# Deformable sampling: gathered rows as TensorE's stationary side against small corner-weight matrices, in place of weighting on VectorE

## Chip, cores, metric

One core of one Trainium2 chip. The metric is the device time of one execution in microseconds (us), the median of several. Every timed execution leaves its span and its mean granted TensorE clock as well. Engines: PE is TensorE's matmul, PEld its weight load, DVE VectorE, ACT ScalarE, POOL GpSimd, SP SyncE. The granted clock is the share of full speed at which TensorE's array was let run, 1 being full speed. In the traces of the kernel before each record of it is 1 or 0.5; other values are means over time. An array at 1 is called warm here, one at 0.5 cold. PSUM is the memory that TensorE writes its sums to; a tile of 128 x 512 float32 in it is called a bank here.

## The reference, cut to what matters

Four images of 256 x 64 x 64 go through four layers, all in float32. Layer 0 is a deformable convolution: for each of 4096 pixels, 4 groups of 64 channels and 9 points, it computes a position, reads the four corners around it, and sums them with bilinear weights and a softmax mask.

```python
def _forward(x, ...):                      # layer 0
    y    = leaky_relu(bn1(conv1x1(x)))
    inp  = y.transpose(0, 2, 3, 1)
    xp   = inp @ inproj_w.T + inproj_b                     # what is sampled
    t    = leaky_relu(bn(depthwise3x3(y)))
    offset, mask = t @ off_w.T + off_b, softmax(t @ mask_w.T + mask_b)   # 9 points a group
    samp = tap(x0, y0, (1-wx)*(1-wy)) + tap(x0+1, y0, wx*(1-wy)) + tap(x0, y0+1, (1-wx)*wy) + tap(x0+1, y0+1, wx*wy)
    dout = (samp * mask).sum(points) @ outproj_w.T + outproj_b
    x2   = bn2(inp + dout)
    ...                                    # squeeze and excitation, feed-forward
# layer 1: linear attention with 5x5 depthwise aggregation; layer 2: 3x3 convolution; layer 3: attention over a pooled image
```

Layer 1's 25-tap aggregation runs on DVE: in layer 1 of the second stage (5,321 to 6,758 us) POOL waits 385.8 us for multiplies on DVE, 77.0 us at the longest, and in seven of the eight longest waits 22 to 33 of the 25-tap instructions run meanwhile.

## The kernel before

The sampling of image n+1 runs beside the later layers of image n: `sample` yields after each tile and the layers yield weights, and so much of the layers is issued beside each tile, in an order that is fixed when the program is built. This is the part that changes (cut):

```python
    def sample(self, n, ssum):
        ...
                for j in range(4):                               # a tile of 128 pixels
                    i = 4 * h + j
                    pd = self.ps2.tile([P, 512], F32, name="pd", tag="ps2")
                    for pr in range(KT):                         # pairs of groups
                        for p3 in range(PT // 3):                # three points at a time
                            g = self.gp.tile([P, 2, 3, 256], F32, name="g", bufs=4)
                            for g2 in range(2):
                                for p in range(3):               # pixels in partitions
                                    nc.gpsimd.indirect_dma_start(out=g[:, g2, p, :], ...)     # L391
                            gw = self.gp.tile([P, 12, 2, 64], F32, name="gw")
                            nc.vector.tensor_tensor(gw..., g..., wt..., ALU.mult)             # L397
                            for q in range(12):
                                nc.tensor.matmul(pd[:, pr * P:(pr + 1) * P],                  # L403
                                                 gw[:, q].rearrange("p g c -> p (g c)"), self.ident, ...)
                    nc.scalar.copy(dT[:, :, j * P:(j + 1) * P], ...)                          # L405
                    yield 1
```

A gather brings the four corners of one point for 128 pixels. DVE multiplies by the weights; TensorE sums, with the weighted rows as the stationary side (loaded as weights) and a 128-column identity as the moving side. A float32 product is recorded as two matmuls with a load each, so the 9,216 products stand in the profile as 18,432.

## Time and profile before

| | before |
|---|---|
| time, median of three runs (lowest to highest) | 12,077.8 us (12,076.2 to 12,086.0) |
| span of the profiled execution | 11,965.6 us |
| PE, DVE, POOL busy | 63%, 52%, 43% |
| mean granted TensorE clock | 0.783 |

The execution of this profile was 112 us shorter than the timed runs.

From the page: busy time by engine, then the span in 40 slices. A digit is the busy share of a slice in tenths (PE), or the granted clock in tenths of full speed (PEclk).

```profile
PE 7491.4 (63%) x32548; PEld 5103.6 (43%) x32548; DVE 6180.6 (52%) x6605; ACT 1463.0 (12%) x2377; POOL 5185.3 (43%) x4614
PE   3545555584366887494557797495546797832696
PEclk6677677796678898696777898697777898965699
```

The clock row is 6 or 7 wherever sampling fills TensorE (0.69 as a mean over image 0's sampling). The stages and waits are in the prediction.

### The profile page before, as it was taken

To read this page: it belongs to the slowest core of one execution; us is meant where nothing else is said; L and a number is where in the kernel's file an instruction comes from. 1 tells how busy PE (TensorE), PEld (TensorE's weight loads), DVE (VectorE), ACT (ScalarE), POOL (GpSimd) and SP (SyncE) were. 2 spreads that over 40 slices of the span, in tenths; PEclk is the share of its full clock that TensorE was granted. 3 is DMA by queue.
4 is the path that set the end of the run, shared out by engine and by line. 5 is a ranking of instruction groups with operands and counts; after the bars stand their busy time and mean duration, and the time that the engine had idled before them with its cause. 6 is when DMAs were issued, how large, how long until landed. Compare 5 with 4: busy or idle time off the path is not lost. (4 is left out here: it accounts for less than half of the span.)

```text
span 11965.6 us, 85517 instructions
## 1 busy us (share of the span) xinstructions
PE 7491.4 (63%) x32548; PEld 5103.6 (43%) x32548; DVE 6180.6 (52%) x6605; ACT 1463.0 (12%) x2377; POOL 5185.3 (43%) x4614
## 2 busy tenths in 40 slices
PE   3545555584366887494557797495546797832696
PEld 2444444353344455353443455344433456421235
DVE  5322222558857233548868323638776423399713
ACT  1000000121010012011100012111110002221002
POOL 0777774355557361445565452245665543000000
PEclk6677677796678898696777898697777898965699
DMA  3333333322222122322221221322222212100000
GB/s 111 109 96 101 97 97 94 103 80 67 65 70 80 53 82 71 114 75 64 67 84 61 67 66 62 110 88 74 74 75 68 76 55 64 56 0 0 0 10 14
DMA packets 451708, 837.94 MB, mean 70 GB/s; under 512 B 222432, under 2 KB 234208, under 8 KB 449504
## 3 DMA queue, kind: packets, MB, share of 16 engines
q0 software_dynamic: 221184, 604.27, 16.7%
q1 hardware_dynamic: 230112, 228.21, 5.9%
q8 instruction: 255, 4.18, 0.1%
q14 instruction: 157, 1.29, 0.0%
HBM read 731.41 MB, written 100.71 MB: 70 GB/s over the span
## 5 line engine op out<-in xcount | busy, mean ns | idle before, releaser
L391 POOL DMA_INDIRECT g<-tab,ixl x4608 | 5184.6, 1125 | 4870.5 <-DVE gw L397 2309.2
L403 PE MATMUL pd<-ident,gw 128*128 128x128 f32 x18432 | 2777.1, 318 | 1545.1 <-DVE gw L397 1019.4
L403 PEld LDWEIGHTS pd<-ident,gw 128*128 128x128 f32 x18432 | 2661.6, 231 | 1727.3 <-DVE gw L397 1052.4
L397 DVE TENSOR_TENSOR gw<-g,wtl 128x1536 f32<-128x1536 f32 x768 | 1348.3, 1758 | 2581.5 <-DMA g<-tab,ixl 1600.0
L150 DVE SCALAR_TENSOR_TENSOR av<-pd,w,av 128x1024 f32<-128x1024 f32 x1152 | 1481.5, 1286 | 1.5
L150 DVE SCALAR_TENSOR_TENSOR ak<-pd,w,ak 128x1024 f32<-128x1024 f32 x1152 | 1480.2, 1285 | 0.4
L606 PE MATMUL ps<-xp,w 128*128 128x512 f32 x2304 | 993.9, 593 | 2.6 <-ACT xp L597 2.6
L521 PE MATMUL pt<-ident,ak 128*128 128x128 f32 x256 | 86.2, 407 | 981.8 <-ACT ak L537 973.8
L606 PEld LDWEIGHTS ps<-xp,w 128*128 128x128 f32 x2304 | 435.3, 189 | 551.8 <-issue 549.2
L405 ACT COPY dT<-pd 128x256 f32<-128x256 f32 x128 | 47.6, 372 | 4113.1 <-PE pd L403 2372.5
L610 DVE TENSOR_TENSOR x<-x,ps 128x512 f32<-128x512 f32 x64 | 44.0, 688 | 878.7 <-PE ps L606 797.1
L456 PE MATMUL ps<-x2f,f 128*128 128x512 f32 x1024 | 468.7, 616 | 40.5 <-ACT hm L457 28.1
L521 PEld LDWEIGHTS pt<-ident,ak 128*128 128x128 f32 x256 | 50.0, 213 | 990.7 <-ACT ak L537 982.1
L462 PE MATMUL ps<-hm,f 128*128 128x512 f32 x1024 | 446.7, 594 | 2.2 <-ACT hm L457 2.2
L313 PE MATMUL ps<-mw,t 128*128 128x108 f32 x512 | 101.0, 378 | 479.8 <-DVE t L134 430.9
L496 PE MATMUL ps<-xn,qw 128*128 128x512 f32 x768 | 379.8, 622 | 11.3 <-ACT xn L116 7.7
L685 PEld LDWEIGHTS ps<-gt,pT 128*128 128x128 f32 x2048 | 294.4, 222 | 110.6 <-issue 52.7
L456 PEld LDWEIGHTS ps<-x2f,f 128*128 128x128 f32 x1024 | 200.4, 198 | 297.0 <-issue 246.6
L685 PE MATMUL ps<-gt,pT 128*128 128x128 f32 x2048 | 298.5, 306 | 37.4 <-DVE pT L682 20.0
L150 DVE SCALAR_TENSOR_TENSOR t<-y,vec,t 128x1024 f32<-128x1024 f32 x256 | 315.7, 1287 | 0.1
L134 DVE SCALAR_TENSOR_TENSOR hm<-hm 128x512 f32<-128x512 f32 x256 | 172.8, 692 | 273.2 <-ACT hm L457 259.2
L668 PE MATMUL s<-ph,th 128*128 128x512 f32 x512 | 312.2, 703 | 0.0
(187 smaller groups left out, 6595.7 us busy)
## 6 DMA issues: line engine op xcount, KB each, us to landing
g<-tab,ixl POOLq DMA_INDIRECT x4608
x<-in_x SPq DMA_DIRECT2D x64, 512.0 KB
tab<-xo SPq DMA_DIRECT2D x512, 64.0 KB
y<-yc SPq DMA_DIRECT2D x32, 512.0 KB
yb<-y SPq DMA_DIRECT2D x32, 512.0 KB
x<-x SPq DMA_DIRECT2D x32, 512.0 KB
x2f<-x SPq DMA_DIRECT2D x32, 512.0 KB
ybf<-y SPq DMA_DIRECT2D x32, 512.0 KB
```

The source lines that it names most:

```text
L134: self.nc.vector.scalar_tensor_tensor(out, z, SLOPE, z, ALU.mult, ALU.max)
L150: nc.vector.scalar_tensor_tensor(acc, s, wt, acc, ALU.mult, ALU.add)
L391: nc.gpsimd.indirect_dma_start(out=g[:, g2, p, :], out_offset=None, in_=table, in_offset=bass.IndirectOffsetOnAxis(ap=ix[:, i, at:at + 1], ...
L397: nc.vector.tensor_tensor(gw.rearrange("p s g c -> p g s c"), g.rearrange("p g q (s c) -> p g (q s) c", c=64), wt[:, i].rearrange("p (g s) ...
L403: nc.tensor.matmul(pd[:, pr * P:(pr + 1) * P], gw[:, q].rearrange("p g c -> p (g c)"), self.ident, start=p3 == 0 and q == 0, stop=p3 == 2 ...
L456: nc.tensor.matmul(ps, f1[:, k, m * P:(m + 1) * P], x2[:, k], start=k == 0, stop=k == KT - 1)
L462: nc.tensor.matmul(ps, f2[:, k, m * P:(m + 1) * P], hm[:, k], start=k == 0, stop=k == 4 * KT - 1)
L496: nc.tensor.matmul(ps, qw[:, k, i * P:(i + 1) * P], xn[:, k], start=k == 0, stop=k == KT - 1)
L521: nc.tensor.transpose(pt[:, 0, j], kv[:, j * P:(j + 1) * P], self.ident)
L606: nc.tensor.matmul(ps, w[:, k, t, m * P:(m + 1) * P], xp[:, k, 8 * b + t // 3:8 * b + t // 3 + 8, t % 3:t % 3 + W], start=i == 0, stop=i = ...
L668: nc.tensor.matmul(s[:, i], tv[:, 4 * b + j], ph[:, i * 512:(i + 1) * 512], start=True, stop=True)
L685: nc.tensor.matmul(ps[:, 0:P], pT[:, m], gt[:, m], start=m == 0, stop=m == 7)
```

## The change

The intent is to take DVE out of the path from a gather to the sum. The samples are laid out by (pixel, point), so that the 128 rows of one gather are some 14 or 15 pixels with 9 points each. The gathered rows, unweighted, become the stationary side. The moving side is a matrix of 128 rows by 32 columns (16 pixels x 2 image rows of the corner): it holds a sample's corner weight in its pixel's column and zero elsewhere. One product then weights and sums. DVE builds only these matrices, which need no gathered data.

```diff
-                            g = self.gp.tile([P, 2, 3, 256], F32, name="g", bufs=4)      # 6 gathers a tile
-                            ... gw = g * wt on DVE, 128 x 1536 ...
-                            for q in range(12):
-                                nc.tensor.matmul(pd[:, pr * P:(pr + 1) * P], gw[:, q]..., self.ident, ...)
+                    wm = self.gp.tile([P, PT, 8, OB], F32, name="wm")                    # OB = 16
+                    nc.vector.tensor_tensor(wm, con("own")..., wt[:, :, 8 * i:8 * i + 8]..., ALU.mult)    # L394
+                    pd = self.ps2.tile([P, 2, 2, P], F32, name="pd", tag="ps2")
+                    for g2 in range(2):
+                        g = self.gp.tile([P, PT, 256], F32, name="g", bufs=4)            # 9 gathers a tile
+                        for j in range(PT):
+                            nc.gpsimd.indirect_dma_start(out=g[:, j, :], ...)            # L404
+                        for j in range(PT):
+                            for x in range(2):
+                                nc.tensor.matmul(pd[:, g2, :, OUT0[j]:OUT0[j] + OB], g[:, j, x * P:(x + 1) * P],   # L409
+                                                 wm[:, j, 4 * g2 + 2 * x:4 * g2 + 2 * x + 2, :], ...)
+                    for s in range(2):
+                        nc.scalar.copy(dT[64 * s:64 * s + 64, ...], pd[64 * s:64 * s + 64, :, s, :])              # L415
```

(Cut: the index and weight layouts in memory, the projection over 4 x 128 rows in place of 2 x 128, buffers merged to make room, and the share of the layers beside a step halved, as a step is half a tile's work.)

More of the change, by code (lines that the diff above doesn't have):

```diff
@@ L27 @@
 SLOPE = 0.01
-SHARE = 56
+SHARE = 28
 EPS_BN = 1e-5
@@ L47 @@
 NVEC = _at
+OB = 16
+OUT0 = [min(P * j // PT, P - OB) for j in range(PT)]
 ROWS = {"inproj_b": (0, C), "offmask_b": (C, 3 * Q), "g_b": (C + 3 * Q, P)}
@@ L52 @@
 CON = {"bd": (0, P), "oh": (P, 16), "bx": (P + 16, Q), "by": (P + 16 + Q, CT * Q),
-       "gi": (P + 16 + Q + CT * Q, Q), "sel": (P + 16 + 2 * Q + CT * Q, 4 * P)}
-NCON = P + 16 + 2 * Q + CT * Q + 4 * P
+       "gi": (P + 16 + Q + CT * Q, Q), "sel": (P + 16 + 2 * Q + CT * Q, 4 * P),
+       "own": (P + 16 + 2 * Q + CT * Q + 4 * P, PT * OB)}
+NCON = P + 16 + 2 * Q + CT * Q + 4 * P + PT * OB
 class Net:
@@ L164, in setup @@
         nc.sync.dma_start(self.rows, a["rows"])
-        self.ow = cp.tile([P, KT, C], F32, name="ow")
+        self.ow = cp.tile([P, G, C], F32, name="ow")
         nc.sync.dma_start(self.ow, a["outproj_wT"])
@@ L179, in setup @@
         self.inv, self.sh = inv, sh
-        self.w5 = cp.tile([P, 6, 25], F32, name="w5")
+        self.w5 = self.vec("dw5", n=150).rearrange("p (m t) -> p m t", t=25)
         nc.vector.tensor_tensor(
-            self.w5, self.vec("dw5", n=150).rearrange("p (m t) -> p m t", t=25),
-            self.vec("agg_pw_w", n=6).unsqueeze(2).to_broadcast([P, 6, 25]), ALU.mult)
+            self.w5, self.w5, self.vec("agg_pw_w", n=6).unsqueeze(2).to_broadcast([P, 6, 25]), ALU.mult)
         self.b5 = cp.tile([P, 6], F32, name="b5")
@@ L193, in setup @@
         self.x2_d = [dt([P, KT, HW], F32, name=f"x2{n}") for n in im]
-        self.w_d = [dt([P, NT, Q * 4], F32, name=f"wt{n}") for n in im]
-        self.i_d = [dt([P, NT, Q], I32, name=f"ix{n}") for n in im]
+        self.w_d = [dt([NCH, P * PT, CT * G * 4], F32, name=f"wt{n}") for n in im]
+        self.i_d = [dt([NCH, P * PT, CT * G], I32, name=f"ix{n}") for n in im]
         self.w2_d = dt([P, KT, 9, C], F32, name="w2")
@@ L342, in coordinates @@
         nc.vector.scalar_tensor_tensor(t1, f0[:, 1], float(TX), f0[:, 0], ALU.mult, ALU.add)
-        ix = bp.tile([P, CT, Q], I32, name="ix")
-        nc.vector.tensor_tensor(ix, tq(t1), self.con("gi").unsqueeze(1).to_broadcast([P, CT, Q]), ALU.add)
-        nc.sync.dma_start(self.i_d[n][:, c * CT:(c + 1) * CT, :], ix)
+        ix = bp.tile([P, PT, CT, G], I32, name="ix")
+        nc.vector.tensor_tensor(
+            ix.rearrange("p q t g -> p t g q"), t1.rearrange("p (t g q) -> p t g q", g=G, q=PT),
+            self.con("gi").rearrange("p (g q) -> p g q", q=PT).unsqueeze(1).to_broadcast([P, CT, G, PT]), ALU.add)
+        nc.sync.dma_start(self.i_d[n][c].rearrange("(p q) f -> p (q f)", q=PT), ix.rearrange("p q t g -> p (q t g)"))
         mg = ml.rearrange("p t (g q) -> p (t g) q", q=PT)
@@ L356, in coordinates @@
         mf = ml.rearrange("p t q -> p (t q)")
-        wt = bp.tile([P, M, 2, 2], F32, name="wt")
+        wt = bp.tile([P, PT, CT * G, 2, 2], F32, name="wt")
+        fq = lambda v: v.rearrange("p (f q) -> p f q", q=PT)
         for xt, wx in ((0, w0[:, 0]), (1, loc[:, 0])):
@@ L361, in coordinates @@
             for yt, wy in ((0, w0[:, 1]), (1, loc[:, 1])):
-                nc.vector.tensor_tensor(wt[:, :, xt, yt], ax, wy, ALU.mult)
-        nc.sync.dma_start(self.w_d[n][:, c * CT:(c + 1) * CT, :].rearrange("p t q -> p (t q)"),
-                          wt.rearrange("p m a b -> p (m a b)"))
+                nc.vector.tensor_tensor(wt[:, :, :, xt, yt].rearrange("p q f -> p f q"), fq(ax), fq(wy), ALU.mult)
+        nc.sync.dma_start(self.w_d[n][c].rearrange("(p q) f -> p (q f)", q=PT),
+                          wt.rearrange("p q f a b -> p (q f a b)"))
     def sample(self, n, ssum):
@@ L372, in sample @@
         for c in range(NCH):
-            ix = sp.tile([P, CT, Q], I32, name="ixl")
-            nc.sync.dma_start(ix, self.i_d[n][:, c * CT:(c + 1) * CT, :])
-            wt = sp.tile([P, CT, 4 * Q], F32, name="wtl")
-            nc.sync.dma_start(wt, self.w_d[n][:, c * CT:(c + 1) * CT, :])
+            ix = sp.tile([P, PT, CT * G], I32, name="ixl")
+            nc.sync.dma_start(ix, self.i_d[n][c].rearrange("(j p) f -> p j f", p=P))
+            wt = sp.tile([P, PT, CT * G * 4], F32, name="wtl")
+            nc.sync.dma_start(wt, self.w_d[n][c].rearrange("(j p) f -> p j f", p=P))
             for h in range(2):
@@ L380, in sample @@
                 nc.sync.dma_start(yb, self.y_d[n][:, :, b * 512:(b + 1) * 512])
-                dT = sp.tile([P, KT, 512], F32, name="dT")
-                for j in range(4):
-                    i = 4 * h + j
-                    pd = self.ps2.tile([P, 512], F32, name="pd", tag="ps2")
-                    for pr in range(KT):
-                        for p3 in range(PT // 3):
-                            g = self.gp.tile([P, 2, 3, 256], F32, name="g", bufs=4)
-                            for g2 in range(2):
-                                for p in range(3):
-                                    at = (2 * pr + g2) * PT + 3 * p3 + p
-                                    nc.gpsimd.indirect_dma_start(
-                                        out=g[:, g2, p, :], out_offset=None, in_=table,
-                                        in_offset=bass.IndirectOffsetOnAxis(ap=ix[:, i, at:at + 1], axis=0))
-                            gw = self.gp.tile([P, 12, 2, 64], F32, name="gw")
-                            at = 12 * p3
-                            nc.vector.tensor_tensor(
-                                gw.rearrange("p s g c -> p g s c"), g.rearrange("p g q (s c) -> p g (q s) c", c=64),
-                                wt[:, i].rearrange("p (g s) -> p g s", g=G)[:, 2 * pr:2 * pr + 2, at:at + 12]
-                                .unsqueeze(3).to_broadcast([P, 2, 12, 64]), ALU.mult)
-                            for q in range(12):
-                                nc.tensor.matmul(pd[:, pr * P:(pr + 1) * P], gw[:, q].rearrange("p g c -> p (g c)"),
-                                                 self.ident, start=p3 == 0 and q == 0, stop=p3 == 2 and q == 11)
-                    nc.scalar.copy(dT[:, :, j * P:(j + 1) * P], pd[:, 0:C].rearrange("p (k t) -> p k t", k=KT))
@@ new lines, in sample @@
+                dT = sp.tile([P, G, 512], F32, name="dT", bufs=1)
+                for i in range(8 * h, 8 * h + 8):
+                    pr, j4 = i % 2, i // 2 % 4
+                    wm = self.gp.tile([P, PT, 8, OB], F32, name="wm")
+                    nc.vector.tensor_tensor(
+                        wm, self.con("own").rearrange("p (j o) -> p j o", o=OB).unsqueeze(2).to_broadcast([P, PT, 8, OB]),
+                        wt[:, :, 8 * i:8 * i + 8].unsqueeze(3).to_broadcast([P, PT, 8, OB]), ALU.mult)
+                    pd = self.ps2.tile([P, 2, 2, P], F32, name="pd", tag="ps2")
+                    for g2 in range(2):
+                        g = self.gp.tile([P, PT, 256], F32, name="g", bufs=4)
+                        for j in range(PT):
+                            at = 2 * i + g2
+                            nc.gpsimd.indirect_dma_start(
+                                out=g[:, j, :], out_offset=None, in_=table,
+                                in_offset=bass.IndirectOffsetOnAxis(ap=ix[:, j, at:at + 1], axis=0))
+                        for j in range(PT):
+                            for x in range(2):
+                                nc.tensor.matmul(pd[:, g2, :, OUT0[j]:OUT0[j] + OB], g[:, j, x * P:(x + 1) * P],
+                                                 wm[:, j, 4 * g2 + 2 * x:4 * g2 + 2 * x + 2, :],
+                                                 start=g2 + j + x == 0, stop=g2 == 1 and j == PT - 1 and x == 1,
+                                                 skip_group_check=True)
+                    for s in range(2):
+                        hs = slice(64 * s, 64 * s + 64)
+                        nc.scalar.copy(dT[hs, 2 * pr:2 * pr + 2, j4 * P:(j4 + 1) * P], pd[hs, :, s, :])
@@ L406, in sample @@
                     yield 1
-                x2 = sp.tile([P, KT, 512], F32, name="x2")
                 for m in range(KT):
                     po = self.ps2.tile([P, 512], F32, name="po", tag="ps2")
-                    for k in range(KT):
-                        nc.tensor.matmul(po, self.ow[:, k, m * P:(m + 1) * P], dT[:, k], start=k == 0, stop=k == KT - 1)
-                    nc.vector.tensor_tensor(x2[:, m], po, yb[:, m], ALU.add)
-                    nc.scalar.activation(x2[:, m], x2[:, m], AF.Identity, bias=self.sh[:, 4 + m:5 + m],
+                    for k in range(G):
+                        nc.tensor.matmul(po, self.ow[:, k, m * P:(m + 1) * P], dT[:, k], start=k == 0, stop=k == G - 1)
@@ L414, in sample @@
+                    nc.vector.tensor_tensor(yb[:, m], po, yb[:, m], ALU.add)
+                    nc.scalar.activation(yb[:, m], yb[:, m], AF.Identity, bias=self.sh[:, 4 + m:5 + m],
                                          scale=self.inv[:, 4 + m:5 + m], accum_out=ssum[:, m, b:b + 1])
-                nc.sync.dma_start(self.x2_d[n][:, :, b * 512:(b + 1) * 512], x2)
+                nc.sync.dma_start(self.x2_d[n][:, :, b * 512:(b + 1) * 512], yb)
     def feedforward(self, n, ssum, x1):
@@ L775, in arrays @@
         "gi": np.broadcast_to((q // PT) * TY * TX + TX + 1, (P, Q)),
+        "own": ((P * np.arange(PT)[None, :, None] + p[:, None, None]) // PT
+                == np.array(OUT0)[None, :, None] + np.arange(OB)[None, None]).reshape(P, -1),
         "sel": (p[:, None, None] == 16 * np.arange(4)[None, :, None] + p[None, None] // 8).reshape(P, -1),
@@ L786, in arrays @@
         "offmask_wT": lhsT(np.concatenate([w[l0 + "off_w"], w[l0 + "mask_w"]])),
-        "outproj_wT": lhsT(w[l0 + "outproj_w"]),
+        "outproj_wT": asc(np.tile(w[l0 + "outproj_w"].T.reshape(G, 64, C).transpose(1, 0, 2), (2, 1, 1))),
         "se_down_wT": lhsT(w[l0 + "se_down_w"]),
```

## The prediction

> **What bounds the kernel now.** I first cut the span into its stages, by where each image's gathers and later layers start and end, and read the busy time of each engine in each. Columns: window, length, busy us and count on PE, PEld, DVE, ACT and POOL, granted clock, DMA share, GB/s.
>
> ```profile
> 233.00:2003.00 1770.00, 891.81 (x4855) 805.90 (x4856) 459.19 (x389) 54.75 (x101) 1253.82 (x1152) 0.69 0.33 99
> 2003.00:2287.00 284.00, 106.30 (x556) 90.62 (x555) 172.25 (x221) 29.73 (x41) 97.98 (x90) 0.66 0.37 117
> 2287.00:4697.00 2410.00, 1671.88 (x7488) 1120.57 (x7488) 1341.83 (x1374) 316.02 (x525) 1214.84 (x1063) 0.82 0.22 68
> 4697.00:5049.00 352.00, 145.63 (x640) 116.64 (x640) 194.28 (x272) 49.74 (x69) 101.61 (x91) 0.69 0.39 125
> 10204.00:11966.00 1762.00, 1091.67 (x3132) 543.95 (x3132) 1023.78 (x1183) 292.55 (x467) 0.00 (x0) 0.78 0.03 11
> ```
>
> Image 0 is sampled with no later layers beside it (1770 us), image 1 is prepared (284), then three times the sampling of an image runs beside the feed-forward and layers 1 to 3 of the one before (2410, 2418, 2391), with a preparation between (352, 346), and the last image's later layers run alone (1762). With the prologue of 233 that is the span of 11,966. The reader is to see that a stage with sampling takes 650 us more than the same layers alone, though no engine is busy more than 70% of it. Next, the layer-1 part of a stage and of the last image, same columns:
>
> ```profile
> 2551.00:3990.00 1439.00, 817.30 (x3991) 594.50 (x3990) 1034.15 (x920) 165.34 (x286) 848.36 (x726) 0.74 0.24 73
> 10438.00:11375.00 937.00, 397.39 (x1029) 178.18 (x1028) 812.17 (x789) 146.30 (x242) 0.00 (x0) 0.64 0.00 2
> ```
>
> 500 of the 650 us are lost there, in a part that is DVE's when alone (812 of 937). Then the waits in the stage from 5049 to 7467 (us in total, times, longest):
>
> ```profile
> POOL g L391 <- DVE gw L397: 676.7, 24, 98.1
> DVE gw L397 <- DMA g<-tab,ixl: 259.7, 54, 7.7
> ```
>
> POOL stops when its four g buffers (24 gathers) are full, because DVE, in order, is deep in 25-tap convolutions; when DVE comes back it needs 36 gathers for a tile, finds 24, and sits idle for the other 12. The two take turns at stalling. Sampling image 0 is different: there POOL issues nearly all the time. Last, the rows of the page and of the timeline that carry the prices:
>
> ```profile
> L391 POOL DMA_INDIRECT g<-tab,ixl x4608 | 5184.6, 1125 | 4870.5 <-DVE gw L397 2309.2
> L403 PE MATMUL pd<-ident,gw 128*128 128x128 f32 x18432 | 2777.1, 318 | 1545.1 <-DVE gw L397 1019.4
> L397 DVE TENSOR_TENSOR gw<-g,wtl 128x1536 f32<-128x1536 f32 x768 | 1348.3, 1758 | 2581.5 <-DMA g<-tab,ixl 1600.0
> ```
>
> ```profile
> 4972.62 0.95 POOL L391 DMA_INDIRECT g<-tab,ixl  x1 [0.30 <-issue]
> 4973.15 1.76 DVE L397 TENSOR_TENSOR gw<-g,wtl 128x1536 f32<-128x1536 f32 x1 [5.45 <-DMA g<-tab,ixl]
> 4973.87 1.86 POOL L391 DMA_INDIRECT g<-tab,ixl  x1 [0.30 <-issue]
> ...
> 4977.69 3.45 PE L313 MATMUL ps<-mw,t 128*128 128x108 f32 x28
> ...
> 4983.28 2.94 PE L403 MATMUL pd<-ident,gw 128*128 128x128 f32 x24 [0.79 <-DVE gw L397]
> ```
>
> A gather costs POOL 0.95 + 0.30 = 1.25 us, and about 0.85 more where a gw multiply meets it.
>
> [...] matmuls with 108 moving columns (28 in 3.45 us, 123 ns) are spaced like those with 128 (24 in 2.94, 122 ns); start to start, taken from the trace, the two common spacings are 112 ns (warm) and 213 (cold) for both. The loads set the pace, not the columns streamed. [...]
>
> **The change, part by part.**
> DVE: 768 multiplies at 1758 ns go (1348 us). 256 products of corner weights with the ownership mask come, 1152 elements each: at 1758/1536 = 1.14 ns an element, 1.32 us, so 338 us in all, 84 an image. More important: they need no gathered data, so DVE no longer waits for a gather or holds its buffers.
> PE: each tile of 128 gathered rows is now the stationary side, 36 products a step, 64 steps an image: 2304, exactly as before (32 x 72), two recorded matmuls each. They stream 32 columns instead of 128, but as the load sets the pace I expect 112/213 ns again and **no gain** on PE: 4608 x 0.112 = 516 us an image warm. The projection contracts over 4 x 128 instead of 2 x 128: 32 recorded matmuls of 430 ns more, +14 us an image.
> ACT: 128 half copies an image instead of 32, about +36 us, unbound.
> POOL: the same 1152 gathers, but a buffer holds 9, four hold 36, and a step needs 18, so two steps are ready in advance instead of two thirds of one. The work beside a step is halved with it. DVE meets POOL 64 times an image instead of 192, for about 0.6 us each: 163 -> 40 us.
> Order: in the built program, image 1's offsets (the L313 group) now stand inside image 0's sampling, not behind it; images 2 and 3 are prepared as before.
>
> Stage by stage:
> - Prologue: 233.
> - Image 0: 1152 x 1.25 = 1440, + 40 for weight products, + 60 for other DVE work in the way, + 65 for the initial and small buffer stalls (49 us before at the start, with 36 gathers ahead about 35) = 1605.
> - Then 35 us to the feed-forward (means and excitation) instead of 284, as offsets and gathers have moved ahead.
> - A stage: the layers alone (222 feed-forward, 937, 266, 325) plus what sampling puts on their bound engine. Counting products in the built order: feed-forward 246 x 2 x 0.112 = +55 -> 277. Layer 1: 40 weight products at 1.35 = 54, + 7 for adds on DVE -> 998; POOL has some 723 gathers to make there, 904 + 40 + 57 of interference = 1000. Two equal chains that feed each other never overlap perfectly, so I add 80 by judgement: 1080 (before 1439). Layer 2: 266 + 23 for its 102 products, + 27 for a cluster of 114 products ahead of it that needs 57 gathers with 36 held -> 315. Layer 3: 325 + 51 + 14, + 40 for a cluster of 132 products -> 430. Sum 2102, say 2105; before 2410. Three: 6315.
> - Two preparations: unchanged at 350, as the feed-forward there stands behind 113 gathers in place of some 75, but fewer stalls: 700.
> - Last image: 1765.
> Sum 233 + 1605 + 35 + 6315 + 700 + 1765 = 10,653; the median before is 112 us over the profile's span: **10,770 us**, 0.89 of before.
>
> **Rivals.**
> (1) The gain is smaller because PE becomes the in-order waiter: it now waits for gathers itself, with the layers' matmuls queued behind. For: clusters of over 100 products between layers; PE busy 817 us in layer 1 at clock 0.74, which does not shrink. Against: 36 gathers in advance. It would leave stages at 2250: 11,200.
> (2) Shorter streams do make PE faster. For: PE busy counts 128 columns. Against: 108 and 128 columns cost the same. At 60 ns a matmul the bound parts would gain some 60 us a stage, and sampling would hold layer 1 less: 10,450.
> (3) Nothing is won, since the gathers bound everything. Against: POOL needs 1152 x 1.27 = 1463 us, far under 2410. It holds for image 0 alone, where the change gives 165 of 1770 us.
> (4) DVE fully decoupled, layer 1 at 1000 or less: 10,500.
>
> **Range and chances.** The 80 us of judgement times three, and rivals 1, 2 and 4, give 10,400 to 11,200. Even with stages only 100 us shorter, the early offsets (250) and image 0 (165) give over 5%, so a miss of the 2% mark would need a new wait nobody sees here. Faster 0.96, same 0.03, slower 0.01.
>
> **What would show it.** Right: the DVE row of 768 replaced by 256 at about 1.3 us; the sampling matmuls still 112/213 ns apart; POOL's wait for a buffer, 677 us a stage, more than halved and put down to PE; DVE no longer waiting for a gather; feed-forward of image 0 starting near 1875 us; stages near 2105 with layer 1 near 1080. Wrong: spacing well under 112 ns (rival 2); PE rows waiting for g by hundreds of us a stage (rival 1); image 0's sampling not near 1605, which would mean that gathers land or issue at another rate in the new row order.

## The result

The changed kernel takes **12,469.0 us** (12,438.1 to 12,500.8, four runs) against 12,079.9 (now four runs): ratio 1.032, 95% interval 1.029 to 1.035. It is slower, where 0.89 had been predicted. The result is correct. (A ratio here is the mean time of one kernel's fast runs over that of the other's in the same rounds, so not quite the ratio of the medians quoted.)

The page of the changed kernel, the same three rows, then the rows of group sums that answer to those in the prediction (line, engine, operation | busy us, mean ns | idle before, and what ended most of it):

```profile
PE 8770.6 (71%) x32804; PEld 6245.6 (50%) x32804; DVE 5211.1 (42%) x6093; ACT 1606.8 (13%) x2761; POOL 5179.5 (42%) x4614
PE   3786667855788873866588986395568897832697
PEclk6555557755667786866566868586656687966698
...
L404 POOL DMA_INDIRECT g<-tab,ixl x4608 | 5178.8, 1124 | 5222.3 <-PE pd L409 2370.4
L409 PE MATMUL pd<-wm,g 128*128 128x32 f32 x18432 | 3599.1, 364 | 1101.5 <-issue 954.3
...
L394 DVE TENSOR_TENSOR wm<-con,wtl 128x1152 f32<-128x1152 f32 x256 | 346.8, 1356 | 2268.5 <-remote 1088.8
```

DVE did what was predicted: 256 operations of 1,356 ns in place of 768 of 1,758, its busy time down by 970 us, and no direct wait for a gather. But PE's busy time is **up** by 1,279 us for the same number of sampling products, and POOL now waits for PE as long (2,370 us) as it waited for DVE before (2,309). The clock row has fives where it had sixes and sevens. And one thing is strange: TensorE stands still for 954 us ahead of sampling products with no recorded cause ("issue"; 467 us before). Part of these 954 us may be waits for gathers all the same, as this trace lacks most of the records of their landing (see the end of the part on why the prediction was wrong).

The same by windows, image 0's sampling and the layer-1 part of the first two stages (columns as in the prediction):

```profile
235.00:2009.00 1774.00, 1211.53 (x5156) 1128.49 (x5157) 362.81 (x464) 116.78 (x230) 1193.78 (x1184) 0.52 0.38 112
2334.00:3826.00 1492.00, 1022.46 (x4000) 767.08 (x3999) 879.56 (x838) 185.82 (x344) 904.09 (x720) 0.61 0.24 69
5328.00:6817.00 1489.00, 1025.61 (x4002) 765.47 (x4001) 879.43 (x838) 186.52 (x344) 900.60 (x720) 0.61 0.24 69
```

The granted clock is 0.52 in the sampling (0.69 before) and 0.61 in layer 1 (0.74). I then counted in the traces how far apart the sampling matmuls start. There are two common spacings in both kernels, 112 and 213 ns, as predicted, but in another mix: 12,701 of 18,432 at the short spacing (under 150 ns) and 4,874 at the long one (150 to 240 ns) before, 4,427 and 12,977 after. The others stand ahead of a wait or at the end of a group. The spacing goes with the granted clock: of the short ones 12,652 and 4,145 start at a clock of 1, of the long ones 4,636 and 12,923 at 0.5.

So there are two suspects, and the prediction had neither:

- **Short streams** (theory A). A product now streams 32 columns. If the array's clock follows the work that streams through it and not the instructions issued, it stays at half speed in the sampling, and products start 213 ns apart in place of 112.
- **Slow stretches** (theory S). In runs of some 4 to 45 us, TensorE starts an instruction (loads and matmuls counted together) only every 0.70 or 1.40 us with no recorded wait. I counted a run of at least five such gaps in close succession. They add up to 343 us before and 1,136 us after, and none comes after the last gather. (The sums shift by some per cent with the rule of counting; a recount gave 335 and 1,106.) Rivals for their cause are TensorE's waits on each gather's own semaphore (S1), or something that does not depend on these waits (S2).

### The profile page after: what moved, and what is told of

The parts are those of the page before. It is cut to its first block, busy times and chain, and to the rows that moved or that the text cites. A ratio compares the mean times of both kernels' runs of the same rounds, so it can differ in the third digit from the quotient of the medians.

```text
span 12436.3 us, 83286 instructions
## 1 busy us (share of the span) xinstructions
PE 8770.6 (71%) x32804; PEld 6245.6 (50%) x32804; DVE 5211.1 (42%) x6093; ACT 1606.8 (13%) x2761; POOL 5179.5 (42%) x4614
## 5 line engine op out<-in xcount | busy, mean ns | idle before, releaser
L404 POOL DMA_INDIRECT g<-tab,ixl x4608 | 5178.8, 1124 | 5222.3 <-PE pd L409 2370.4
L409 PE MATMUL pd<-wm,g 128*128 128x32 f32 x18432 | 3599.1, 364 | 1101.5 <-issue 954.3
L409 PEld LDWEIGHTS pd<-wm,g 128*128 128x128 f32 x18432 | 3631.9, 298 | 1240.2 <-issue 1060.0
L155 DVE SCALAR_TENSOR_TENSOR av<-pd,vec,av 128x1024 f32<-128x1024 f32 x1152 | 1481.3, 1286 | 1.9
L155 DVE SCALAR_TENSOR_TENSOR ak<-pd,vec,ak 128x1024 f32<-128x1024 f32 x1152 | 1480.1, 1285 | 0.4
L394 DVE TENSOR_TENSOR wm<-con,wtl 128x1152 f32<-128x1152 f32 x256 | 346.8, 1356 | 2268.5 <-remote 1088.8
L415 ACT COPY dT<-pd 64x256 f32<-64x256 f32 x512 | 187.8, 367 | 5177.7 <-PE pd L409 2413.1
L420 PE MATMUL po<-dT,ow 128*128 128x512 f32 x512 | 316.5, 769 | 230.3 <-ACT dT L415 178.8
L505 PE MATMUL ps<-xn,qw 128*128 128x512 f32 x768 | 411.1, 665 | 4.5 <-ACT xn L121 4.4
L689 PE MATMUL pt<-ident,pe 128*128 128x128 f32 x1024 | 166.6, 311 | 299.9 <-ACT pe L683 287.3
L581 PE MATMUL rden<-rd,con 64*128 64x512 f32 x256 | 241.6, 1041 | 153.5 <-DVE rd L575 100.5
```

The source lines that it names most:

```text
L155: nc.vector.scalar_tensor_tensor(acc, s, wt, acc, ALU.mult, ALU.add)
L394: nc.vector.tensor_tensor(wm, self.con("own").rearrange("p (j o) -> p j o", o=OB).unsqueeze(2).to_broadcast([P, PT, 8, OB]), wt[:, :, 8 * ...
L404: nc.gpsimd.indirect_dma_start(out=g[:, j, :], out_offset=None, in_=table, in_offset=bass.IndirectOffsetOnAxis(ap=ix[:, j, at:at + 1], axi ...
L409: nc.tensor.matmul(pd[:, g2, :, OUT0[j]:OUT0[j] + OB], g[:, j, x * P:(x + 1) * P], wm[:, j, 4 * g2 + 2 * x:4 * g2 + 2 * x + 2, :], start=g ...
L420: nc.tensor.matmul(po, self.ow[:, k, m * P:(m + 1) * P], dT[:, k], start=k == 0, stop=k == G - 1)
L505: nc.tensor.matmul(ps, qw[:, k, i * P:(i + 1) * P], xn[:, k], start=k == 0, stop=k == KT - 1)
```

## The experiments

Eighteen runs were made, each on one chip with timed runs of the kernel before beside it. I call the chips A to E. They turned out to be of two kinds: on A and D every kernel with its gathers has slow stretches; on B (where e5 alone has all its gathers), C and E none has a single one. The first result's traces have them. So I compare within a chip, or by ratio among chips of one kind.

| run | kernel | chip | us | before there | ratio (95%) | warm / cold sampling matmuls | stretches, us |
|---|---|---|---|---|---|---|---|
| e1 | before, 32 columns | A | 12,325 | 12,111 | 1.016 (1.012-1.021) | 6,276 / 11,326 | 602 |
| e2 | after, PSUM split, 32 columns | A | 12,586 | 12,111 | 1.039 (1.036-1.042) | 4,926 / 12,503 | 1,167 |
| e3 | same, 64 columns | A | 12,230 | 12,111 | 1.010 (1.007-1.012) | 8,189 / 8,813 | 1,354 |
| e4 | same, 100 columns | A | 11,956 | 12,111 | 0.987 (0.984-0.990) | 13,271 / 3,222 | 1,584 |
| e5 | after, 4 of 36 products | B | 10,437 | 11,425 | 0.914 (0.912-0.915) | - | 0 |
| e6 | after, 1 gather of 9 | B | 11,015 | 11,425 | 0.964 (0.962-0.966) | 3,594 / 14,799 | 0 |
| e7 | 100 columns, 1 gather of 9 | B | 9,139 | 11,425 | 0.800 (0.799-0.801) | 17,230 / 1,083 | 0 |
| e8 | before, 1 gather of 6 | B | 9,461 | 11,425 | 0.828 (0.827-0.829) | 17,171 / 1,129 | 0 |
| e9 | before | C | 11,441 | 11,440 | 1.000 (0.998-1.002) | 11,609 / 6,185 | 0 |
| e10 | after | C | 11,246 | 11,440 | **0.983** (0.981-0.984) | 5,033 / 12,266 | 0 |
| e11 | 100 columns | C | 10,358 | 11,440 | **0.905** (0.904-0.907) | 11,794 / 4,346 | 0 |
| e12 | 100 columns, copied | C | 10,824 | 11,440 | 0.946 (0.944-0.948) | 12,631 / 5,147 | 0 |
| e13 | after | D | 12,411 | 11,985 | 1.036 (1.033-1.039) | 4,679 / 12,727 | 1,120 |
| e14 | 100 columns | D | 11,893 | 11,985 | 0.994 (0.990-0.998) | 13,608 / 3,020 | 1,470 |
| e15 | 100 columns, copied | D | 11,948 | 11,985 | 0.998 (0.995-1.001) | 13,364 / 3,499 | 1,532 |
| e16 | before, 32 columns | E | 11,825 | 11,448 | 1.032 (1.031-1.034) | 6,072 / 11,898 | 0 |
| e17 | after, split, 32 columns | E | 11,271 | 11,448 | 0.985 (0.983-0.986) | 5,229 / 12,147 | 0 |
| e18 | split, 64 columns | E | 10,852 | 11,448 | 0.948 (0.946-0.949) | 8,768 / 7,330 | 0 |

"Warm" is under 150 ns to the next matmul, "cold" 150 to 240. By the 2% mark of the record e3, e4, e9, e10, e14, e15 and e17 count as the same as before, and e1 is unclear; a smaller difference is called one here only where its interval leaves out 1. e1, e16 and e5 to e8 are wrong; the others are correct.

### e1 to e4: does the number of streamed columns set the pace of the loads?

e1 is the kernel before with the identity cut to 32 columns in 35 of 36 products of each sum; stationary side, loads, DVE and gathers stay. The order in which the built program issues its work did not stay, as the traces show: the second image's offsets moved into image 0's sampling, as they did in the changed kernel, and the first feed-forward starts at 2,085 us in place of 2,287.

```diff
                             for q in range(12):
+                                cols = P if p3 == 0 and q == 0 else 32
-                                nc.tensor.matmul(pd[:, pr * P:(pr + 1) * P], gw[:, q]..., self.ident, ...)
+                                nc.tensor.matmul(pd[:, pr * P:pr * P + cols], gw[:, q]..., self.ident[:, 0:cols], ...)
```

> The kernel before, in which 35 of 36 sampling products of a pair of groups stream 32 columns of the identity instead of 128 (the result is wrong on purpose); order, waits, gathers and DVE are as before. Theory A (short streams leave the array at half clock, so a weight load takes 213 ns instead of 112): most sampling matmuls move to 213 ns, the granted clock while sampling image 0 falls from 0.69 to about 0.55, and the time rises by 2 to 6% (12,300 to 12,800 us). Theory B (the loss comes from the new order and the waits of PE for single gathers): spacing and time as before, 12,000 to 12,150 us. Theory C (loads do not set the pace): faster.

e2 is the changed kernel with a PSUM bank for each of the two groups' sums. That leaves half a bank free, into which e3 and e4 stream useless copies of each product:

```diff
-                    pd = self.ps2.tile([P, 2, 2, P], F32, ...)      # both groups in one bank
                     for g2 in range(2):
+                        pd = self.ps2.tile([P, 512], F32, ...)      # sum in columns 0 to 255
 ...
+                            reps = 1                                # e2;  e3: 2;  e4: 2 if b0 < 32 else 3 if b0 < 144 else 4
+                            rhs = wm[...].unsqueeze(1).to_broadcast([P, reps, 2, OB])
+                            out = [..., [step, reps], ...]          # copies land in columns 256 to 511, never read
```

> A control for the next two: the changed kernel with one PSUM bank for each group's sum instead of one for two (three banks for sampling, three for the rest), still 32 columns. A and B: near the changed kernel, 12,300 to 12,700 us, clock near 0.69, spacing mostly 213 ns.

> The control with each product streamed twice over (64 columns, the second copy into columns that nobody reads); same result. A: if half the load's time in streaming is enough for full clock, as the next run, else as the control. B: as the control, never better by over 2%.

> The control with each product streamed two to four times over (64 to 128 columns, 100 in the mean), same result. A: the clock rises to 0.75 or more, most sampling matmuls are 112 ns apart, and the time falls to between 10,700 and 11,700 us. B: as the control or slower, since only useless work was added.

Measured: shortening the kernel before turns its mix over (12,701 warm to 6,276) and costs 1.6% net, just under the 2 to 6% expected; the moved offsets had given some 200 us back, so the short streams cost more than that. Lengthening the changed kernel's streams with columns that nobody reads raises the warm matmuls from 4,926 through 8,189 to 13,271 and the clock from 0.686 through 0.72 to 0.767, and the time falls with it, by 5% in all. More work on TensorE made the kernel faster, which of these theories only A expects. What it is in a stream that counts (columns read, or results written) these runs do not separate. But e4 missed the 10,700 to 11,700 us that A gave it, and is still 1,190 us over my 10,770, with more stretches than ever. Something else was at work.

### e5 to e8: products without gathers, gathers without products

With e4 left unexplained, theory A had to stand against a theory B: the gathers' traffic itself holds the other engines up. e5 keeps all gathers and all weight matrices but only 4 of 36 products a step. e6 and e7 keep all products but gather one block of nine, which all products read; e8 does the same to the kernel before (one gather of six, read by the whole multiply).

```diff
-                        for j in range(PT):
-                            for x in range(2):
+                            for x in range(2):       # e5: over all 128 pixels, from g[:, 0]
 ...
-                        for j in range(PT):          # gathers
+                        for j in range(1):           # e6, e7; products read g[:, 0]
```

> Wrong result on purpose: the changed kernel with all 4,608 gathers and all of VectorE's corner-weight matrices, but 4 instead of 36 products a tile (each over all 128 pixels). What is left open by the first four runs is why the version with a warm array (11,956 us) still has layer 1 at 1,450 us and image 0's sampling at 1,765 us. Theory A, the time of TensorE in its fixed order is what the sampling costs a stage: with 32 of 36 products gone, image 0's gathers run at 1.25 us each and end near 1,700 us, a stage falls to what the last image takes alone plus the preparation (1,755 + 350 = 2,105 us) plus little, and the whole to 10,300 to 10,700 us. Theory B, the gathers' traffic itself holds the other engines up: the products matter little, stages stay above 2,350 us and the whole above 11,500 us. Under both, the slow stretches of TensorE are not needed to explain anything if A's number comes out.

> Wrong result on purpose: the changed kernel with all products and matrices, but one gather in place of nine (512 instead of 4,608), all products reading it. Theory A: image 0's sampling is no longer held to 1.25 us a gather but to TensorE's 4,608 instructions at about 0.2 us plus the next image's preparation beside it, so it falls from 1,791 to about 1,200 us; the stages stay near 2,500 us because TensorE's load is the same; the whole is 11,500 to 11,900 us. Theory B: the stages fall to 2,150 us too and the whole to under 10,900 us. The stretches in which TensorE starts an instruction only every 0.7 us (1,136 us in all in the changed kernel) vanish if gathers cause them.

> Wrong result on purpose: the version with further copies of each product (100 columns on average, warm array) with one gather in place of nine. Theory A: about 11,956 less 500 us for image 0, so 11,200 to 11,500 us, and the stages stay near 2,430 us. Theory B: under 10,500 us, with stages near 2,150 us and no slow stretches of TensorE.

> Wrong result on purpose: the kernel before with one gather in place of six (768 instead of 4,608), VectorE's weighting reading that row for all. If gathers are what both kernels wait for, it is VectorE's weighting (1,536 operations of 1,536 elements) that then costs here, and the changed kernel without gathers should be faster than this one, as its VectorE work is a quarter. If TensorE's order and clock decide (theory A), this one stays faster than the changed kernel with one gather, by about 300 us: near 11,200 to 11,500 us against 11,500 to 11,900 us.

Measured, the layer-1 part of one stage, e5, e6, e7 and e8 in this order (columns as before):

```profile
4446.00:5545.00 1099.00, 516.23 (x1445) 262.50 (x1444) 884.68 (x839) 184.90 (x345) 746.69 (x711) 0.68 0.32 93
...
4650.00:5904.00 1254.00, 978.53 (x3966) 734.38 (x3965) 869.11 (x837) 184.33 (x342) 366.15 (x79) 0.63 0.05 15
...
3570.00:4575.00 1005.00, 719.92 (x3997) 527.33 (x3996) 870.68 (x838) 198.94 (x423) 481.93 (x80) 0.82 0.06 19
...
3678.00:4782.00 1104.00, 711.06 (x3986) 517.29 (x3985) 1020.21 (x920) 163.51 (x285) 223.53 (x121) 0.80 0.07 23
```

e5's total met theory A's number, but not its parts: a stage with its preparation took 2,413 and 2,400 us (A: 2,105 and a little), and layer 1, with nearly all products gone, still 1,099 us against 937 alone. e6 fell between the two, with stages of 2,180 us, near what B had written. e7 and e8 fell far under A's numbers. That is in part because I had written all of them in the times of chip A, and the kernel before is 6% faster on B; so e5's hit is luck in part, and only the order of the four is a test. (Whether the stretches vanish without gathers could not be tested on B, as e5 has none with them.) There A holds for e6 against e8 (by 1,554 us, five times what it expected), and B for e7 against e8. Both have a share. Three readings hold whatever the stretches are, as chip B has none:

- The DVE saving is real. With few gathers and a warm array, e7 beats e8 by 322 us, and by 100 us in layer 1: DVE has 871 us there in place of 1,020.
- The cold array is costly. e6 and e7 have the same gathers and the same DVE work and differ in the columns streamed (and in the split, worth nothing by e17): 11,015 against 9,139 us. In layer 1 the clock is 0.63 against 0.82, PE is busy 979 us against 720, and the part takes 1,254 us against 1,005.
- Keeping TensorE busy without a pause did not warm it here, with streams of 32 columns. A group of products of e6, in order of time (start us, us, ..., count):

```profile
6224.66 16.19 PE L409 MATMUL pd<-wm,g 128*128 128x32 f32 x75
```

75 matmuls in 16.19 us, 216 ns each, with nothing between them. The granted clock shows the array falling asleep at work. This group starts at 6216.5 us, right behind matmuls of 512 columns and at full clock, and loses it 4 us later though TensorE never pauses (columns as before, the clock third from the end):

```profile
6216.50:6220.30 3.80, 3.80 (x36) 3.77 (x34) 3.50 (x6) 0.00 (x0) 0.94 (x1) 1.00 0.51 138
6220.30:6240.70 20.40, 20.40 (x98) 20.40 (x97) 8.69 (x16) 0.98 (x3) 1.90 (x3) 0.50 0.07 20
```

### e9 to e12: the same kernels on a chip without stretches

As the kernel before took 12,111 us on chip A and 11,425 on B, I ran it, the changed kernel and e4's kernel again, with a trace each, on one chip. e12 tests S1: ScalarE copies each block of nine gathers to a second tile, and TensorE reads that, so its products wait once for ScalarE and no longer for each gather.

```diff
-                        g = self.gp.tile([P, PT, 256], F32, name="g", bufs=4)
+                        g = self.gp.tile([P, PT, 256], F32, name="g", bufs=2)
 ...
+                        gc = self.gp.tile([P, PT, 256], F32, name="gc", bufs=2)
+                        nc.scalar.copy(gc, g)
-                                nc.tensor.matmul(out, g[:, j, x * P:(x + 1) * P], ...
+                                nc.tensor.matmul(out, gc[:, j, x * P:(x + 1) * P], ...
```

> A control: the kernel before itself, for its trace on the chip that the next three run on. The first four runs had a chip where it takes 12,111 us, the second four one where it takes 11,425 us. If the slow stretches of TensorE (343 us in the trace of the kernel before) are what differs between chips, this trace has more of them where its time is longer; ratio to itself 1.00.

> A control: the changed kernel itself on the same chip. By the first result its ratio is 1.03. Both theories of its remaining cost (waits on gathers, or traffic) expect slow stretches of TensorE of about 1,100 us if the chip is like the first, fewer on one like the second.

> A control: the version with further copies of each product (100 columns) on the same chip, for its trace beside the next one; ratio 0.987 as on the first chip, slow stretches about 1,600 us on such a chip.

> Correct result. The 100-column version, but ScalarE copies each block of nine gathers to a second tile (two buffers of each in place of four of the gathers), and TensorE reads the copy: its products then wait once for ScalarE and no longer for every gather's own semaphore; gathers and their traffic stay. Theory S1, TensorE's waits on the gathers' semaphores make its slow stretches: they fall from about 1,600 us to the 343 us of the kernel before or less, and the time falls to 0.91 to 0.95 of before. Theory S2, the gathers' traffic holds up what TensorE itself has to fetch: the stretches stay above 1,000 us and the time is within 3 per cent of the version without the copy, or longer, as fewer gathers can run ahead.

Measured: chip C has no stretch in any of them, so e12 could not decide (there the copy only costs: 0.946 against 0.905). But the comparison is clean now, and it reads otherwise than the first result: the changed kernel is 1.7% **faster** than before (the interval is 0.981 to 0.984), and with a warm array 9.5% faster. Image 0's sampling and layer 1 of a stage, for e9 (before), e10 (after) and e11 (100 columns):

```profile
234.00:1889.00 1655.00, 953.85 (x4852) 883.27 (x4853) 458.67 (x388) 54.13 (x100) 1249.17 (x1152) 0.73 0.34 105
5029.00:6390.00 1361.00, 804.55 (x3990) 594.12 (x3989) 1033.02 (x920) 163.66 (x286) 847.26 (x726) 0.75 0.25 77
```

```profile
235.00:1762.00 1527.00, 1293.74 (x5156) 1124.57 (x5157) 363.42 (x464) 116.83 (x230) 1140.05 (x1160) 0.53 0.44 128
4756.00:6039.00 1283.00, 999.77 (x3999) 744.24 (x3998) 881.50 (x838) 185.72 (x343) 907.54 (x720) 0.64 0.28 80
```

```profile
234.00:1780.00 1546.00, 1214.75 (x5163) 982.95 (x5163) 363.99 (x465) 136.61 (x358) 1160.74 (x1158) 0.66 0.43 127
4447.00:5604.00 1157.00, 833.54 (x3997) 594.01 (x3996) 883.10 (x838) 198.68 (x423) 865.33 (x720) 0.76 0.30 89
```

In layer 1 DVE has 150 us less than before in both of the new ones. With the cold array PE has 195 us more, and only 78 us of the stage's part are won; warm, 204. A group of sampling products between layers 2 and 3, of e10 and of e11, shows the two speeds in place (54 in 11.71 us is 217 ns each, 81 in 9.23 is 114):

```profile
6394.81 11.71 PE L409 MATMUL pd<-wm,g 128*128 128x32 f32 x54
```

```profile
5909.74 9.23 PE L423 MATMUL pd<-wm,g 128*128 128x96 f32 x81
```

And what a stretch is, in the timeline of PE at the start of image 0's sampling, the first result's trace of the changed kernel and then e10, the same kernel on chip C (start us, us, ..., idle before and its cause):

```profile
433.04 0.21 PE L409 MATMUL pd<-wm,g 128*128 128x32 f32 x1 [1.21 <-issue]
435.14 0.21 PE L409 MATMUL pd<-wm,g 128*128 128x32 f32 x1 [1.89 <-issue]
437.24 0.21 PE L409 MATMUL pd<-wm,g 128*128 128x32 f32 x1 [1.88 <-issue]
439.34 0.21 PE L409 MATMUL pd<-wm,g 128*128 128x32 f32 x1 [1.89 <-issue]
```

```profile
422.07 1.06 PE L409 MATMUL pd<-wm,g 128*128 128x32 f32 x4 [0.28 <-DMA g<-tab,ixl]
423.36 1.06 PE L409 MATMUL pd<-wm,g 128*128 128x32 f32 x4 [0.23 <-DMA g<-tab,ixl]
424.66 3.45 PE L409 MATMUL pd<-wm,g 128*128 128x32 f32 x12 [0.24 <-DMA g<-tab,ixl]
428.38 2.23 PE L409 MATMUL pd<-wm,g 128*128 128x32 f32 x8 [0.26 <-DMA g<-tab,ixl]
```

On C, TensorE takes four matmuls for each gather as it lands. In the stretch one matmul starts every 2.1 us (three times 0.70), with nothing recorded to wait for.

### e13 to e15: are the stretches TensorE's waits on the gathers?

The same kernels as e10, e11 and e12, on one more chip.

> The changed kernel itself on one more chip. If the chip shows the slow stretches: ratio to before 1.03 and stretches of about 1,100 us. If not: 0.98 and none.

> The 100-column version on the same chip: 0.987 with stretches of about 1,600 us, or 0.905 without.

> The 100-column version whose products read ScalarE's copy of the gathers. On a chip without the stretches 0.946, as it was. On a chip with them: if TensorE's waits on the gathers' semaphores make them (S1), they fall from about 1,600 us to under 350 us and the ratio is below 0.97; if they do not depend on those waits (S2), they stay above 1,000 us and the ratio is above 1.00.

Measured: chip D has the stretches, so the copy could be put to the test. It leaves them where they were, 1,532 us against 1,470, and the time too (0.998 against 0.994; S2 had expected a little over 1.00). S1 is refuted: e15's products wait on no gather, and still, in a stretch of its timeline:

```profile
370.91 0.32 PE L425 MATMUL pd<-wm,gc 128*128 128x96 f32 x1 [2.07 <-issue]
371.64 0.32 PE L425 MATMUL pd<-wm,gc 128*128 128x96 f32 x1 [0.42 <-issue]
374.44 0.32 PE L425 MATMUL pd<-wm,gc 128*128 128x96 f32 x1 [2.48 <-issue]
```

The changed kernel's first result is confirmed on D (1.036).

### e16 to e18: the columns again, without stretches

Kernels of e1, e2 and e3 on chip E, which has no stretches.

> Wrong result on purpose: the kernel before with 35 of 36 products a sum streaming 32 of the identity's columns. On a chip with the slow stretches 1.016 as before. On one without them, if short streams alone cost what they cost the changed kernel (8 per cent between 100 and 32 columns there): 1.05 to 1.08.

> The changed kernel with one PSUM bank for each group's sum, 32 columns. With stretches 1.04. Without them: if the split by itself is worth nothing, 0.98 to 0.99, like the changed kernel there; if the split is what made the 100-column version fast, 0.92 or less.

> The same with every product streamed twice, 64 columns. With stretches 1.01. Without them, if the time follows the columns: half way between 0.983 and 0.905, so 0.93 to 0.96.

Measured: the split by itself is worth nothing (0.985 against the 0.983 of e10), 64 columns give 0.948, and 100 gave 0.905 on C. So the ratio follows the columns. e16 costs 3.2%, less than the 5 to 8% I expected. Part of the reason is in its order: as in e1, the edit let the second image's offsets move into image 0's sampling, and the feed-forward starts at 1,938 us in place of 2,161 (in e9, on C). Its later stages are 2,431 to 2,433 us against e9's 2,265 to 2,271, so a cold array costs the old kernel some 165 us a stage.

The 100-column version is the fastest correct kernel seen here: it beats the changed kernel on every chip on which both ran, and the kernel before by 9.5% on C, 1.3% on A and 0.6% on D.

## Why the prediction was wrong

The stages by the traces, in us. "Prep" are the preparations of images 2 and 3; a chip with stretches is the first result's (before, after) and D (100 columns), one without is C.

| stage | predicted | before, with | after, with | 100 col., with | before, without | after, without | 100 col., without |
|---|---|---|---|---|---|---|---|
| prologue | 233 | 233 | 235 | 236 | 234 | 235 | 234 |
| image 0's sampling | 1,605 | 1,770 | 1,774 | 1,747 | 1,655 | 1,527 | 1,546 |
| to its feed-forward | 35 | 284 | 17 | 29 | 272 | 19 | 29 |
| three stages, each | 2,105 | 2,410 / 2,418 / 2,390 | 2,637 / 2,591 / 2,565 | 2,422 / 2,461 / 2,407 | 2,273 / 2,265 / 2,271 | 2,369 / 2,304 / 2,300 | 2,051 / 2,021 / 2,022 |
| layer 1 in each | 1,080 | 1,439 / 1,437 / 1,413 | 1,492 / 1,489 / 1,477 | 1,401 / 1,477 / 1,427 | 1,365 / 1,361 / 1,364 | 1,286 / 1,283 / 1,284 | 1,156 / 1,157 / 1,158 |
| prep, each | 350 | 352 / 346 | 421 / 427 | 397 / 388 | 343 / 342 | 362 / 363 | 345 / 343 |
| last image | 1,765 | 1,746 | 1,753 | 1,756 | 1,746 | 1,752 | 1,756 |

**The step that failed** is the one on PE: "as the load sets the pace I expect 112/213 ns again and no gain on PE: 4608 x 0.112 = 516 us an image warm". The two spacings were right. What I took over without saying so was the share of each. I had noted that loads set the pace, had a granted clock of 0.69 in image 0's sampling and of 0.64 in layer 1 alone (PE busy 397 of 937 us) before me, and did not join the two: if the spacing of 112 ns needs a warm array, and 96 of 128 streamed columns go, it may not stay warm. It did not. The matmuls at the short spacing fell from 12,701 to 4,427 of 18,432. The columns bring it back in both kinds of chip, and the time with it (e2 to e4; e17, e18, e11).

**What that was worth.** On chip C, from e10 to e11: 0.983 to 0.905, 888 us; on D, with stretches, from e13 to e14: 1.036 to 0.994, 518 us. e11 has about the array that I assumed (11,794 warm matmuls), and its stages come to 2,051, 2,021 and 2,022 against the predicted 2,105, its preparations to 345 and 343 against 350, image 0's sampling to 1,546 against 1,605. Its ratio of 0.905 is near the 0.89 predicted. So the rest of the sum held in total, but partly by luck. Errors had opposite signs: layer 1 is 1,157 and not 1,080, and layer 3 is 322 and not 430. The sum was built from a trace with stretches and met on a chip without them. And the 112 us added at its end, for the profile of the kernel before being shorter than the timed runs, was a difference between executions and no cost.

**What was left in layer 1.** Two things in the traces, neither tested by a run. First, DVE was not set free from the gathers. The weight matrix `wm` has two buffers, and a buffer comes free only when the products that read it are done, which wait for gathers. So DVE waits for PE where it had waited for gathers. DVE's longest wait of this kind in layer 1 of a stage, e9 and then e10 (us, times, longest):

```profile
DVE gw L397 <- DMA g<-tab,ixl: 250.4, 49, 7.8
DVE wm L394 <- PE pd L409: 112.7, 10, 19.8
```

In e11 it is 91.2 us. Second, the prediction had DVE's hindrance of POOL fall from 163 to 40 us an image, but a gather's mean did not move (1,125 to 1,124 ns). Beside weight products there is less of it: 632 gathers ran beside `gw` multiplies and nothing else of DVE's before, 141 beside `wm` products after, with means of 1.36 and 1.34 us. In its place, fifteen gathers of the changed kernel's first trace took 13.8 to 49.5 us each, 471 us over the usual 0.95 in all, every one of them beside a run of 25-tap instructions; the longest gather before took 5.2 us. Most gathers beside these instructions are not held: 753 of the 839 that ran beside 25-tap instructions alone took under 1 us before, 652 of 802 after. What picks those that are held no run here shows. A held one in e10 (start us, us):

```profile
2288.15 42.33 POOL L404 DMA_INDIRECT g<-tab,ixl  x1 [0.30 <-issue]
2330.78 2.16 POOL L404 DMA_INDIRECT g<-tab,ixl  x1 [0.30 <-issue]
```

Behind it TensorE takes single gathers as they land, from 2329.70 us on. In e11 there are two such gathers a stage, 44.7 and 51.9 us, both in layer 1.

**What the stretches were worth.** The prediction knew only 112 and 213 ns; on chips A and D there is a third pace, one start every 0.70 or 1.40 us. The kernel before has it as well (343 us in its trace), but the changed kernel over three times as much. From C to D the kernel before loses 545 us and the changed one 1,165, which is what turns 0.983 into 1.036. This is across chips; that the stretches are the cause is argued from their size and place, and no run on one chip switched them off. What makes them stays open. It is not TensorE's waits on gathers (e15). They appear only beside gathers. And those traces record fewer landings: e10's has 73,698 for 4,608 gathers, 16 each, and of as many the changed kernel's first trace holds 21,749 (and the kernel before's 30,628). That the recording itself paces TensorE on such chips is a guess of mine and not shown: every timed execution here was recorded as well, and no run without it exists.

**The signs named in the prediction, one by one.**

- The DVE row: 256 at 1,356 ns. Right; and no DVE wait for a gather. Right by name; in effect DVE still waits behind them, through PE.
- Offsets moved into image 0's sampling, the feed-forward soon after it: 17 to 29 us for 272 to 284. Right, and worth about 250 us on both kinds of chip. On C that is more than the changed kernel's whole gain (194 us). It comes from the order of the built program and not from the products as such: e1 and e16 have it with the old products.
- POOL's wait for a buffer more than halved, and put down to PE. It went to PE, and shrank little. POOL's waits within one stage, for e9 (before), e10 (after) and e11 (100 columns), us, times, longest:

```profile
POOL g L391 <- DVE gw L397: 567.7, 21, 84.7
```

```profile
POOL g L404 <- PE pd L409: 518.7, 18, 168.4
```

```profile
POOL g L404 <- PE pd L423: 369.6, 17, 125.4
```

- Stages near 2,105, layer 1 near 1,080, image 0's sampling near 1,605, feed-forward near 1,875. All wrong in the first result (2,026 for the last); with a warm array and no stretches 2,021 to 2,051, 1,157, 1,546 and 1,809.

**The rivals.** Rival 1 came in half: TensorE did become the engine that the others wait for, but not because it waits for gathers (e10's page has 308 us of that before all sampling matmuls, some 77 an image); it was slow at its own work. Rival 2 had the sign wrong: shorter streams made each product slower and not faster (a recorded sampling matmul took 318 ns in the mean before and 364 after). Rival 3 is refuted as a bound by e6 and e11. Rival 4 was not reached.

## What to carry to other kernels

Where matmuls with fewer columns start no closer together (112 and 213 ns for 108 columns as for 128), the columns streamed look free. Here they were not: with the same gathers, 32 columns gave 14,799 sampling matmuls at the cold spacing and a clock of 0.63 in layer 1 (e6), 100 columns 1,083 and 0.82 (e7). Before shortening a stream, compare the granted clock and the mix of spacings with it, and if the mix would tip, try filling the stream (even with columns that nobody reads) before giving the idea up. And when two chips differ by 6% on the same kernel, take a trace on each before explaining a few per cent: here the sign of the change depended on the chip.
